# Reordering the places of an attention layer from chunk, head, node to head, node, chunk, with output products of 40 columns

## The chip, the cores and the metric

The kernel runs on one core of a Trainium2 chip. The time of a run is the device time in microseconds of one execution of the whole program. Four runs of the kernel before the change took 7528.65, 7554.27, 7571.19 and 7575.57 us, with a median of 7562.73 us.

## The reference

The program computes four graph layers with normalizations and residuals on 6250 nodes and 100,000 edges, all in fp32. Edges are sorted by destination. The change touches only layer 0, the attention layer, whose core is this (cut):

```python
msg_s = (s_n @ Ws_src)[src] + (s_n @ Ws_dst)[dst]
msg_v = einsum(v_n, Wv_src)[src] + einsum(v_n, Wv_dst)[dst]
w1 = rbf @ W_rbf
m1_s, m1_v = _cg_tp(msg_s, msg_v, y0, y1, w1...)
a = leaky(m1_s @ W_alpha), per head: sum(a * alpha_dot)
ex = exp(a - segment_max(a, dst)[dst])
den = segment_sum(ex, dst); alpha = ex / den[dst]
val_s, val_v = gated projections of m1_s, m1_v
m2_s, m2_v = _cg_tp(val_s, val_v, y0, y1, w2...)
h = per head: [m2_s @ Ws_vlin, m2_v @ Wv_vlin]       # 16 + 8*3 = 40 numbers of each head
agg = segment_sum(alpha * h, dst)
```

A message is formed for each edge, each of 4 heads scores it, and each destination node takes a softmax over its edges and adds up the 40 numbers of each head with the weights of the softmax.

## The kernel before

Edges are cut into 784 chunks of 128; 4 chunks are one window, so there are 196 windows (class `Window0`, from L1545). As edges are sorted, the destinations of a chunk lie within 16 consecutive nodes from a base node that is known per chunk (`WM0 = 16`). A pair of chunks uses the 128 partitions as *places*: one partition for each combination of chunk of the pair (2), head (4) and node (16). Before the change partition 64 x chunk + 16 x head + node is the place, so a chunk has a contiguous half (`S = 64`).

What one window goes through, with the lines that matter here:

- **Loads.** The base nodes of the chunks are read into registers of SyncE (`bases`). The rows of their 16 destination nodes (`nodes`, L1584, tile `fw`) come by four DMAs, one for each chunk, to the first 16 rows of a quarter of 32 partitions. Rows of the source nodes come by indirect DMAs from GpSimd (L978, tile `f`). For groups of four windows, `ends_load` brings the destination numbers (tile `dn`) on SyncE's queue, and `radial_load` brings the radial inputs (tiles `yr`, `yb`) on ScalarE's queue.
- **Masks.** `masks` compares the destination numbers with the node of each place (`on`, 1 where the edge belongs to the place).
- **Messages.** `ends` (L1602) multiplies the mask of a chunk, 16 rows of it, with its 16 node rows: this spreads node rows over edges, into PSUM tile `wf`. `weights` (L1607) puts the radial weights beside them. `features` and the four pieces of `product1` (L1623, L1625, L1627, L1629, all on VectorE, reading `wf`) form the tensor product `tp`.
- **Projections.** `turn` transposes (L1650) into a PSUM bank `m` (four such banks rotate), `turned` copies (ScalarE, L1655, tile `xt`), `linear` multiplies (L1662), `tanh`, `directed`, `gates`, `values`, `gated`, `crossed` and `joined` make the values `val`.
- **Scores.** `channels` (L1720), `leak`, `leaky`, `scores` (L1733) with the matrix `adot` give every place a score for every edge. `largest` (VectorE, L1742) takes the maximum over edges; the tile `row` (42 numbers for each place and pair) starts here. `exps` (ScalarE, L1758, one instruction for each pair) makes the weights `pT`, with places on partitions and edges along the free axis. `denominators` (VectorE, L1765) adds them up into column 40 of `row`.
- **Sums.** `by_edge` (L1771) transposes the weights so that edges are on partitions. `weighted` (VectorE, L1778, tile `py`) multiplies them with the four spherical harmonics. `sums` (L1786) multiplies with the scalar values, `sums_z` (L1799) with the vector values, and `summed` (ScalarE, L1791, twice, tile `a`) and `summed_z` (ScalarE, L1807, tile `az`) copy the results to SBUF, channels on partitions and places along the free axis.
- **Outputs.** `outputs` (L1818) applies the last linear map for each pair: 5 groups of channels times 4 blocks of 32 places, so 20 fp32 products for a pair and 40 for a window. Each works on 32 columns of the array, has 32 places of `a` or `az` as the loaded weights, and streams `w_o`. A block of 32 places holds two heads, so `w_o` has 80 columns, 40 for each, and half of the 80 results are of the wrong head.
- **Rows.** `even` (ScalarE, L1823) and `odd` (VectorE, L1827) pick the right 40 by multiplying with a mask `own` and its complement. `write` (SyncE, L1841) stores the 64 partitions of a chunk to a table in HBM, where later code merges the chunks.

An fp32 product appears in the trace as two passes: two records of a weight load (LDWEIGHTS) and two of a product (MATMUL).

The order of the work is written by hand. Stage s of the loop goes through the list `STEP0` (L1899 to L1913) and does every operation named there for window s - lag, in a block in which the program's order is kept on each engine:

```python
for lag, name, *arg in STEP0:
    if 0 <= s - lag < NST:
        getattr(ws[s - lag], name)(*arg)
fill()
```

`fill` issues one DMA of zeros for later tables at the end of a stage. SyncE's queue in a stage is: register loads, node rows, the loads of `ends_load` (every fourth stage), then the four `write`s and `fill`. [...]

Of the kernel before, what the change touches and what calls it, by code (L numbers as in the profile page):

```python
# [48 lines left out]
def kernel(ctx: ExitStack, tc: tile.TileContext, t: dict, out: bass.AP):  # L49
# [230 lines left out]
    slot0 = const.tile([P, 2], F32, name="slot0")  # L280
    win0B = const.tile([1, NW0], I32, name="win0B")
    lane0 = const.tile([P, 1], F32, name="lane0")
    with tc.tile_pool(name="win", bufs=1) as sb, tc.tile_pool(name="winp", bufs=1, space=PSUM) as ps:
# [155 lines left out]
        vec.tensor_scalar(bits[:, 0:1], pi, 15, None, ALU.bitwise_and)  # L439
        vec.tensor_scalar(bits[:, 1:2], pi, 6, None, ALU.logical_shift_right)  # L440
        vec.tensor_scalar(bits[:, 2:3], pi, 5, 1, ALU.logical_shift_right, ALU.bitwise_and)
        vec.tensor_scalar(bits[:, 3:4], pi, 4, 1, ALU.logical_shift_right, ALU.bitwise_and)
        bf = sb.tile([P, 4], F32, name="bf")
        vec.tensor_copy(bf, bits)
        vec.tensor_scalar(bf[:, 2:3], bf[:, 2:3], 2.0, bf[:, 3:4], ALU.mult, ALU.add)
        vec.tensor_scalar(slot0[:, 0:1], bf[:, 1:2], float(WM0), bf[:, 0:1], ALU.mult, ALU.add)
        vec.tensor_scalar(slot0[:, 1:2], bf[:, 2:3], float(NROWS), slot0[:, 0:1], ALU.mult, ALU.add)
        bd = sb.tile([P, NCH], F32, name="bd")
# [6 lines left out]
        for g in range(4):  # L455
            q = slice(32 * g, 32 * g + 32)
            vec.tensor_copy(win0F[q, :], nb[q, g // 2 : NCH : 2])
# [1089 lines left out]
    class Window0:  # L1547
# [12 lines left out]
        def __init__(self, w, sb, ps, n, k, radial, dst, gi, y, yc, ids, node_idx, rows, tps):  # L1560
            self.w, self.sb, self.ps, self.n, self.np = w, sb, ps, n, n // 2
            self.k, self.radial, self.dst = k, radial, dst
            self.gi, self.y, self.yc, self.ids, self.node_idx = gi, y, yc, ids, node_idx
            self.rows, self.tps = rows, tps
            self.first, self.radial_next = True, None
            self.t, self.z, self.pa = {}, {}, {}
            self.f = self.xt = self.th = self.q = self.val = self.a = self.pz = self.po = None

            self.groups = [(g, c) for g, c in enumerate(ORDER0) if c < n]
# [7 lines left out]
        def nodes(self):  # L1577

            self.fw = self.sb.tile([P, F], F32, name="fw", bufs=4)
            if self.rows is None:  # L1580
                gather(self.fw, feat[1][:, :], self.node_idx)
                return
            for g, c in self.groups:
                nc.sync.dma_start(self.fw[32 * g : 32 * g + WM0, :], feat[1][ds(self.base[c], WM0), :])  # L1584
# [11 lines left out]
        def ends(self):  # L1596
# [3 lines left out]
            for g, c in self.groups:  # L1600
                q = slice(32 * g, 32 * g + WM0)
# [151 lines left out]
        def exps(self, old=None):  # L1753
# [3 lines left out]
            for p in range(self.np):  # L1757
                act.activation(self.pT[:, p, :], s[:, p, :], AF.Exp, bias=neg[:, p : p + 1])  # L1758
# [3 lines left out]

        def denominators(self):
            m = self.np
            vec.tensor_reduce(self.row[:, 0:m, 40], self.pT[:, 0:m, :], AX.X, ALU.add)  # L1765

        def by_edge(self):

            self.pe = self.bank()
            for p in range(self.np):  # L1770
                pe.transpose(self.pe[:, p * P : (p + 1) * P], self.pT[:, p, :], ident)  # L1771
# [16 lines left out]
        def summed(self, p):  # L1788
            if self.a is None:
                self.a = self.sb.tile([P, 2, 2, 8, 32], F32, name="a", bufs=2)  # L1790
            act.copy(self.a[:, p], self.pa[p].rearrange("p (h k m) -> p h k m", h=2, k=8))  # L1791
# [11 lines left out]
        def summed_z(self):  # L1803
            m = self.np
            self.az = self.sb.tile([P, 2, 4, 32], F32, name="az", bufs=2)
            z = self.pz[:, 0 : 4 * S].rearrange("p (h k m) -> p h k m", h=2, k=4)[:, :, 0 : 2 * m]
            act.copy(self.az[:, :, 0 : 2 * m], z)  # L1807

        def outputs(self, p):

            w = self.w["o"]
            if self.po is None:
                self.po = self.bank()[:, 0:160].rearrange("p (a k) -> p a k", a=2)
            for i in range(5):
                for r in range(4):
                    h, g = r // 2, r % 2
                    x = self.a[:, p, h, 2 * i + g] if i < 4 else self.az[:, h, 2 * p + g]
                    pe.matmul(self.po[32 * r : 32 * r + 32, p, :], x, w[:, i, g, :], start=i == 0, stop=i == 4)  # L1818

        def even(self):  # L1820

            m = self.np
            act.activation(self.row[:, 0:m, 0:40], self.po[:, 0:m, 0:40], AF.Copy, scale=self.w["own"][:, 0:1])  # L1823

        def odd(self, old=None):
            m, row = self.np, self.row
            vec.scalar_tensor_tensor(  # L1827
                row[:, 0:m, 0:40], self.po[:, 0:m, 40:80], self.w["own"][:, 1:2], row[:, 0:m, 0:40], ALU.mult, ALU.add
            )
            if old is not None:  # L1830
                vec.scalar_tensor_tensor(row[:, 0, 0:41], old[:, 0:41], self.keep, row[:, 0, 0:41], ALU.mult, ALU.add)
# [7 lines left out]
        def write(self, c):  # L1839
            k, h = self.rows[0][c], c % 2  # L1840
            nc.sync.dma_start(tabs[0][k][0][:, ds(self.base[c], WM0), :], self.row[h * S : (h + 1) * S, c // 2, :])  # L1841
# [42 lines left out]
    class Ends:  # L1884
# [5 lines left out]
        def load(self):  # L1890
            n = self.dst[0].shape[1]
            self.dn = self.sb.tile([P, self.m, P], self.dst[0].dtype, name="dn", bufs=2)
            for h in range(2):
                nc.sync.dma_start(self.dn[h * S : (h + 1) * S, 0:n, :], self.dst[h].to_broadcast([S, n, P]))
# [4 lines left out]
        (3, "dots"), (3, "dot", 1), (1, "edges", 0), (3, "dot", 2), (1, "edges", 1), (0, "bases"), (0, "nodes"),  # L1899
# [3 lines left out]
        (4, "turned", 0), (8, "outputs", 0), (4, "tanh", 3), (3, "product1", 1), (8, "even"), (3, "product1", 2),  # L1903
        (4, "channels"), (5, "gates"), (4, "leak"), (3, "product1", 3), (4, "directed", 3), (0, "ends_load"),
        (2, "ends"), (5, "crossed"), (5, "joined", 0), (0, "edges", 2), (5, "joined", 1), (0, "edges", 3), (8, "odd"),
# [535 lines left out]
```

## Time and profile before

One execution was profiled. Its span is the time from the first to the last instruction of the trace.

| what | value |
|---|---|
| median of four runs | 7562.73 us |
| profiled execution | 7578.01 us |
| its span | 7576.2 us |
| TensorE products, busy | 6278.6 us (83%) |
| VectorE busy | 5082.5 us (67%) |
| ScalarE busy | 3030.6 us (40%) |
| GpSimd busy | 4214.0 us (56%) |
| mean granted clock of TensorE | 0.874 |
| loop of layer 0, outputs (L1818) of first and last window | 343.8 to 2461.5 us of the span |
| distance of the outputs of neighbouring stages | 10.9 us |

PE stands for TensorE's products, PEld for its weight loads, which overlap them, DVE for VectorE, ACT for ScalarE, POOL for GpSimd and SP for SyncE. A line of the timeline or of the groups names the line of the program, the operation, its output and inputs by tile name, then the sizes; for TensorE "128\*32 128x80" means rows by columns of the array that are used and the moving data's partitions by columns. "x32" counts instructions. A "<-" in a wait names what ended it; "issue" is time in which the engine waited for nothing that the profile shows.

### The profile page before, as it was taken

The numbers are of one execution on the slowest core, as the hardware profiler recorded it, in microseconds if no ns is written. First come the engines' busy times: TensorE is split into PE (matmuls) and PEld (weight loads), VectorE is DVE, ScalarE is ACT, GpSimd is POOL, SyncE is SP. The second block draws the span as 40 slices with busy tenths as digits, with TensorE's granted clock in tenths as the row PEclk, the third lists the DMA queues.
The fourth block names the chain that finished last, engine by engine and source line by source line (L and its number), as shares of the span: only waits on it lengthen the run. The fifth ranks groups of instructions, "written<-read, shape, count | busy, mean of one in ns | idle before, by whom it ended". The sixth has DMA issues, their size and how long they took to land. (4 is left out here: it accounts for less than half of the span.)

```text
span 7576.2 us, 188755 instructions
## 1 busy us (share of the span) xinstructions
PE 6278.6 (83%) x69706; PEld 4869.4 (64%) x69706; DVE 5082.5 (67%) x12849; ACT 3030.6 (40%) x8425; POOL 4214.0 (56%) x4019
## 2 busy tenths in 40 slices
PE   1799999999999799999999567777777677777776
PEld 0687878878888688888888444444455444444454
DVE  5688889888988788888888544444444334444444
ACT  0455555555555566666666421111111101111112
POOL 0355655655554387877888435545454345454443
PEclk9999999999999899999999767777777777777777
DMA  4444444444432677777777633333333333333333
GB/s 139 123 104 101 103 101 105 102 102 105 102 86 52 131 134 124 128 127 124 129 123 116 177 93 99 87 101 91 101 92 102 95 90 111 94 110 94 109 101 91
DMA packets 772958, 814.43 MB, mean 107 GB/s; under 512 B 187424, under 2 KB 634529, under 8 KB 770337
## 3 DMA queue, kind: packets, MB, share of 16 engines
q1 hardware_dynamic: 498016, 504.14, 22.5%
q0 software_dynamic: 225792, 269.95, 21.5%
q10 hardware_dynamic: 48192, 27.91, 1.5%
q8 instruction: 562, 9.21, 0.5%
q14 instruction: 396, 3.24, 0.1%
HBM read 524.80 MB, written 276.70 MB: 106 GB/s over the span
## 5 line engine op out<-in xcount | busy, mean ns | idle before, releaser
L978 POOL DMA_INDIRECT f<-feat,r_src x2352 | 2322.4, 987 | 1959.7 <-issue 503.2
L1397 POOL DMA_INDIRECT tab<-o,scat x784 | 1385.2, 1767 | 429.9 <-issue 111.1
L1130 PE MATMUL pa<-pr,oy 128*32 128x160 f32 (+4 forms) x15680 | 998.3, 294 | 621.3 <-issue 609.5
L1130 PEld LDWEIGHTS pa<-pr,oy 128*32 128x32 f32 x15680 | 600.0, 123 | 1121.4 <-issue 1050.4
L1096 DVE TENSOR_TENSOR wy<-ww,r_y 128x576 f32<-128x576 f32 x131 | 99.0, 756 | 836.6 <-PE ww L1070 503.7
L1104 DVE TENSOR_TENSOR pr<-f,ww 128x384 f32<-128x384 f32 x131 | 72.5, 553 | 863.7 <-PE ww L1070 614.1
L1662 PE MATMUL m<-w_m,xt 128*128 128x128 f32 x4704 | 622.9, 276 | 0.7 <-DVE q L1679 0.4
L1662 PEld LDWEIGHTS m<-w_m,xt 128*128 128x128 f32 x4704 | 588.4, 192 | 11.7 <-ACT xt L1655 1.1
L1136 ACT COPY o<-pa 128x160 f32<-128x160 f32 x262 | 76.5, 292 | 1136.3 <-remote 710.9
L1070 PE MATMUL ww<-w,hid 64*128 64x192 f32 (+1 forms) x2088 | 448.0, 485 | 96.7 <-issue 68.5
L1655 ACT COPY xt<-m 128x384 f32<-128x384 f32 x784 | 356.6, 481 | 413.8 <-PE m L1771 166.8
L1640 POOL TENSOR_TENSOR d<-d 128x128 f32<-128x128 f32 x392 | 203.1, 518 | 499.1 <-DVE d L1636 495.0
L1366 ACT COPY xt<-pt 128x384 f32<-128x384 f32 x784 | 374.5, 482 | 196.1 <-PE pt L1364 168.4
L1138 ACT COPY o<-pa 128x96 f32<-128x96 f32 x262 | 62.2, 237 | 963.3 <-remote 679.7
L1070 PEld LDWEIGHTS ww<-w,hid 64*128 64x128 f32 x2088 | 276.8, 255 | 210.6 <-issue 180.1
L1786 PE MATMUL m<-py,val 128*128 128x256 f32 x1568 | 403.8, 380 | 0.0
L1364 PE MATMUL pt<-ident,tp 128*128 128x128 f32 x2352 | 388.1, 273 | 16.7 <-DVE tp L975 16.0
L1818 PE MATMUL m<-w_o,a 128*32 128x80 f32 x12544 | 351.1, 235 | 61.1 <-issue 61.1
L1374 PE MATMUL lin<-l,xt 128*128 128x160 f32 x1568 | 386.5, 328 | 0.0
L1354 ACT COPY fw<-pf 128x384 f32<-128x384 f32 x784 | 337.8, 484 | 113.8 <-PE pf L1352 96.5
L1650 PE MATMUL m<-ident,tp 128*128 128x128 f32 x2352 | 376.6, 283 | 1.9 <-ACT xt L1655 1.7
L1070 PE MATMUL ww<-w2z,hid 128*128 128x192 f32 (+1 forms) x1048 | 353.7, 471 | 8.4 <-issue 8.1
(424 smaller groups left out, 15229.8 us busy)
## 6 DMA issues: line engine op xcount, KB each, us to landing
tab<-zeros SPq DMA_DIRECT2D x170, 448.0 KB
nodes<-in_src_row_dram SPq DMA_DIRECT2D x392, 128.0 KB
f<-feat,r_src POOLq DMA_INDIRECT x2352
tb<-tab SPq DMA_DIRECT2D x20, 1288.0 KB
tb<-tab SPq DMA_DIRECT2D x20, 1280.0 KB
dn<-in_dst_row_dram SPq DMA_DIRECT2D x98, 256.0 KB
dn<-in_dst_row_dram SPq DMA_DIRECT2D x196, 128.0 KB
e<-in_ef64T_dram SPq DMA_DIRECT2D x196, 128.0 KB
```

Of the source, the lines that this page charges most:

```text
L978: pool.indirect_dma_start(out=o, out_offset=None, in_=table, in_offset=bass.IndirectOffsetOnAxis(ap=idx, axis=0),)
L1070: pe.matmul(self.ww[:, q, 0:wn], self.hid[k, c * P : (c + 1) * P], m, start=True, stop=True)
L1130: pe.matmul(o, self.oy[:, q, r], x, start=c + piece == 0, stop=c == self.ns[h] - 1 and piece == len(ps_) - 1)
L1364: pe.transpose(pt[:, k, :], self.tp[:, c, k * P : (k + 1) * P], ident)
L1366: act.copy(self.xts[c], pt)
L1374: pe.matmul(z[:, 64:224], xt[:, 2, :], w["l3"], start=True, stop=False)
L1397: pool.indirect_dma_start(out=self.tables[c % len(self.tables)], out_offset=bass.IndirectOffsetOnAxis(ap=self.scat[:, c : c + 1], axis=0), ...
L1650: pe.transpose(pt[:, k * P : (k + 1) * P], self.tp[:, c, k * P : (k + 1) * P], ident)
L1655: act.copy(self.xt[:, :, c, :], self.t[c][:, 0 : 3 * P].rearrange("p (k e) -> p k e", k=3))
L1662: pe.matmul(z[:, k, :], self.xt[:, k, c, :], self.w["m"][:, k, :], start=True, stop=True)
L1786: pe.matmul(pa[:, h * 256 : (h + 1) * 256], self.val[:, c, 0:P], py, start=True, stop=True)
L1818: pe.matmul(self.po[32 * r : 32 * r + 32, p, :], x, w[:, i, g, :], start=i == 0, stop=i == 4)
```

## The change

Places are put in the order head, node, chunk: partition 32 x head + 2 x node + chunk of the pair. A block of 32 places now belongs to one head, with the two chunks of the pair side by side.

- `outputs`: `w_o` is [128, 5, 4, 40] in place of [128, 5, 2, 80]. The number of products stays at 40 for each window; each streams 40 columns. The results are already the right ones, so `even` becomes a plain copy, `rows_out`, and `odd` and `own` go.
- `denominators` goes; `exps` has ScalarE's exponentials add up along the free axis as they run (`accum_out`).
- The transposes of `by_edge` store their columns in the order chunk, head, node, as what follows expects. `summed` and `summed_z` store places with chunks interleaved, so every second element.
- `ends` uses all 32 rows of a quarter. `fw` becomes four fixed tiles, set to zero once; the node rows of a chunk go to every second partition. `write` and the loads of `ends_load` address every second partition as well.
- In `STEP0`, `bases` and `nodes` move from the front of the list to behind `ends_load` and `radial_load`.
- Preparation: positions of the places are worked out anew (`slot0`, `win0F`), and `adot` is put together by two VectorE copies in place of two DMAs.

The code below is the core of the diff; a path for windows left over after the loop changes in the same way and is left out.

```diff
         def nodes(self):
...
+            self.fw = next(self.fws)
             for g, c in self.groups:
-                nc.sync.dma_start(self.fw[32 * g : 32 * g + WM0, :], feat[1][ds(self.base[c], WM0), :])
+                nc.sync.dma_start(
+                    self.fw[32 * g + c % 2 : 32 * g + 32 : 2, :], feat[1][ds(self.base[c], WM0), :]
+                )
...
             for g, c in self.groups:
-                q = slice(32 * g, 32 * g + WM0)
+                q = slice(32 * g, 32 * g + 32)
                 pe.matmul(self.wf[:, c, 0:F], self.on[q, c // 2, :], self.fw[q, :], start=True, stop=True)
...
-                act.activation(self.pT[:, p, :], s[:, p, :], AF.Exp, bias=neg[:, p : p + 1])
+                act.activation(
+                    self.pT[:, p, :], s[:, p, :], AF.Exp, bias=neg[:, p : p + 1], accum_out=self.row[:, p, 40:41]
+                )
...
-        def denominators(self):
-            m = self.np
-            vec.tensor_reduce(self.row[:, 0:m, 40], self.pT[:, 0:m, :], AX.X, ALU.add)
-
         def by_edge(self):
 
             self.pe = self.bank()
             for p in range(self.np):
-                pe.transpose(self.pe[:, p * P : (p + 1) * P], self.pT[:, p, :], ident)
+                o = self.pe[:, p * P : (p + 1) * P].rearrange("q (h m) -> q m h", h=2)
+                pe.transpose(o, self.pT[:, p, :], ident)
...
         def summed(self, p):
             if self.a is None:
-                self.a = self.sb.tile([P, 2, 2, 8, 32], F32, name="a", bufs=2)
-            act.copy(self.a[:, p], self.pa[p].rearrange("p (h k m) -> p h k m", h=2, k=8))
+                self.a = self.sb.tile([P, 2, 16, 32], F32, name="a", bufs=2)
+            o = self.a[:, p].rearrange("p k (n h) -> p h k n", h=2)
+            act.copy(o, self.pa[p].rearrange("p (h k n) -> p h k n", h=2, k=16))
...
         def summed_z(self):
             m = self.np
-            self.az = self.sb.tile([P, 2, 4, 32], F32, name="az", bufs=2)
-            z = self.pz[:, 0 : 4 * S].rearrange("p (h k m) -> p h k m", h=2, k=4)[:, :, 0 : 2 * m]
-            act.copy(self.az[:, :, 0 : 2 * m], z)
+            self.az = self.sb.tile([P, 8, 32], F32, name="az", bufs=2)
+            z = self.pz[:, 0 : 4 * S].rearrange("p (h k n) -> p h k n", h=2, k=8)[:, :, 0 : 4 * m]
+            act.copy(self.az[:, 0 : 4 * m].rearrange("p k (n h) -> p h k n", h=2), z)
...
-                self.po = self.bank()[:, 0:160].rearrange("p (a k) -> p a k", a=2)
+                self.po = self.bank()[:, 0:80].rearrange("p (a k) -> p a k", a=2)
             for i in range(5):
                 for r in range(4):
-                    h, g = r // 2, r % 2
-                    x = self.a[:, p, h, 2 * i + g] if i < 4 else self.az[:, h, 2 * p + g]
-                    pe.matmul(self.po[32 * r : 32 * r + 32, p, :], x, w[:, i, g, :], start=i == 0, stop=i == 4)
-
-        def even(self):
+                    x = self.a[:, p, 4 * i + r] if i < 4 else self.az[:, 4 * p + r]
+                    pe.matmul(self.po[32 * r : 32 * r + 32, p, :], x, w[:, i, r, :], start=i == 0, stop=i == 4)
+
+        def rows_out(self):
 
             m = self.np
-            act.activation(self.row[:, 0:m, 0:40], self.po[:, 0:m, 0:40], AF.Copy, scale=self.w["own"][:, 0:1])
-
-        def odd(self, old=None):
-            m, row = self.np, self.row
-            vec.scalar_tensor_tensor(
-                row[:, 0:m, 0:40], self.po[:, 0:m, 40:80], self.w["own"][:, 1:2], row[:, 0:m, 0:40], ALU.mult, ALU.add
-            )
...
+            act.copy(self.row[:, 0:m, 0:40], self.po[:, 0:m])
...
-            nc.sync.dma_start(tabs[0][k][0][:, ds(self.base[c], WM0), :], self.row[h * S : (h + 1) * S, c // 2, :])
+            nc.sync.dma_start(tabs[0][k][0][:, ds(self.base[c], WM0), :], self.row[h:P:2, c // 2, :])
...
-                nc.sync.dma_start(self.dn[h * S : (h + 1) * S, 0:n, :], self.dst[h].to_broadcast([S, n, P]))
+                nc.sync.dma_start(self.dn[h:P:2, 0:n, :], self.dst[h].to_broadcast([S, n, P]))
...
     STEP0 = [
-        (3, "dots"), (3, "dot", 1), (1, "edges", 0), (3, "dot", 2), (1, "edges", 1), (0, "bases"), (0, "nodes"),
+        (3, "dots"), (3, "dot", 1), (1, "edges", 0), (3, "dot", 2), (1, "edges", 1),
...
-        (4, "turned", 0), (8, "outputs", 0), (4, "tanh", 3), (3, "product1", 1), (8, "even"), (3, "product1", 2),
+        (4, "turned", 0), (8, "outputs", 0), (4, "tanh", 3), (3, "product1", 1), (8, "rows_out"), (3, "product1", 2),
...
-        (2, "ends"), (5, "crossed"), (5, "joined", 0), (0, "edges", 2), (5, "joined", 1), (0, "edges", 3), (8, "odd"),
-        (0, "radial_load"), (2, "weights"), (3, "turn", 3), (8, "write", 0), (4, "leaky"), (6, "by_edge"),
-        (3, "turned", 3), (4, "linear", 0), (7, "sums", 1), (4, "tanh", 0), (7, "denominators"), (7, "summed", 1),
+        (2, "ends"), (5, "crossed"), (5, "joined", 0), (0, "edges", 2), (5, "joined", 1), (0, "edges", 3),
+        (0, "radial_load"), (0, "bases"), (0, "nodes"), (2, "weights"), (3, "turn", 3), (8, "write", 0), (4, "leaky"), (6, "by_edge"),
+        (3, "turned", 3), (4, "linear", 0), (7, "sums", 1), (4, "tanh", 0), (7, "summed", 1),
```

## The prediction

> **What bounds the kernel now.** I looked first at the clock and the busy shares of long windows, to see which part of the span the change can reach. Columns: window, its length, then busy time with number of instructions for TensorE products (PE), weight loads (PEld), DVE, ACT and POOL, then the granted TensorE clock, the DMA share and GB/s.
>
> ```profile
> 500.00:2400.00 1900.00, 1837.62 (x31133) 1520.82 (x31127) 1703.51 (x5359) 1069.78 (x3285) 1128.40 (x1427) 1.00 0.42 98
> ...
> 2462.00:7576.00 5114.00, 4088.17 (x33897) 3054.34 (x33897) 2987.48 (x6190) 1764.13 (x4563) 2928.50 (x2352) 0.82 0.49 110
> ```
>
> The loop of layer 0 fills the first window and ends at 2461.5 us; all that the change touches, but for some preparation, is there: 196 stages of about 10.9 us, 28% of the span. The second window is code that stays as it is, so I cost it at nothing. In the loop PE is busy 97% (1837.6 of 1900), DVE 90%, ACT 56%, at full clock. PE looks like the bound, but a busy PE is not a PE at its peak, so the waits in the same window come next (engine, tile, line <- what ended the wait: total us, times, longest).
>
> ```profile
> ACT row L1823 <- PE m L1818: 270.0, 172, 1.9
> ...
> PEld m L1818 <- issue: 116.7, 346, 0.8
> ...
> DVE py L1778 <- PE m L1771: 102.4, 150, 0.9
> ...
> PE m L1818 <- issue: 56.2, 173, 0.6
> ```
>
> TensorE stops once in every stage (173 stages) inside the output products, L1818, and no semaphore ends the stop. The timeline of one stage shows where (start, length, engine, ..., idle before).
>
> ```profile
> 1408.97 0.59 ACT L1791 COPY a<-m 128x512 f32<-128x512 f32 x1 [0.52 <-PE m L1786]
> ...
> 1409.86 0.76 PE L1818 MATMUL m<-w_o,a 128*32 128x80 f32 x32
> ...
> 1410.44 0.32 PE L1818 MATMUL m<-w_o,az 128*32 128x80 f32 x8
> ...
> 1410.58 0.31 PE L1818 MATMUL m<-w_o,a 128*32 128x80 f32 x4
> 1410.63 0.55 DVE L1627 TENSOR_TENSOR tp<-f,wf 128x384 f32<-128x384 f32 x1
> ...
> 1411.24 0.71 PE L1818 MATMUL m<-w_o,a 128*32 128x80 f32 x26 [0.36 <-issue]
> ...
> 1412.08 0.65 PE L1720 MATMUL m<-xt,w_alpha 128*64 128x256 f32 x4
> ```
>
> Of the 80 passes (40 fp32 products of two passes), 44 run by 1410.65, nothing starts until 1411.24, then 36 run. Over some 155 stages the restart comes 0.07 us after the end of DVE's L1627, with nine stages in ten inside a band of 0.08 us, while its distance from the products' own start spreads from 1.21 to 1.48 us (10th to 90th percentile). So the restart goes with the DVE chain, not with how soon the first 44 passes are done. No wait of the program says so; I don't know the mechanism, and that is the largest doubt here. With it the stage is a loop: L1720 at 1401.16, the transposes L1771, DVE's py L1778 at 1403.78 (2.62 later), a chain of DVE work without a gap to the end of L1627 at 1411.17 (7.39), restart, 36 passes and the change of tile shape to L1720 at 1412.08 (0.91): 10.92 us.
>
> **The change part by part.**
>
> *Output products, 80 to 40 columns.* The number of passes and weight loads stays. The price per pass I take from two groups of the same shape of weights (128*32). The first 32 passes of the outputs above take 0.76 us with the last pass's own 0.235: (0.76 - 0.235)/31 = 16.9 ns from start to start. For 64 columns there is L1799:
>
> ```profile
> 1416.19 0.65 PE L1799 MATMUL m<-py,val 128*32 128x64 f32 x32
> ```
>
> (0.65 - 0.222)/31 = 13.8 ns. So 3.1 ns for 16 columns, 0.19 ns per column, and 40 columns would be 9.3 ns if the line holds that far. Were all 80 passes on the path, this gives 80 x 7.6 = 0.61 us per stage, 119 us. But by the loop above only the 36 after the restart are. They take 0.68 us from first start to last. The first four come about 20 ns apart, as the queue fills again, and I leave those 0.08; the other 32 take 0.30 at 9.3 ns (gain 0.30), 0.44 at the 13.8 ns that the trace has shown to be possible (gain 0.16), and 0.51 at 16 ns, the pace of the weight loads just after the restart (gain 0.09). I take 0.22, between the first two: 196 x 0.22 = **43 us**. Bounds in this case: 18 to 59 us.
>
> [...]
>
> *Work taken from DVE.* L1765 (414 ns) and L1827 (298 ns) go: 0.71 us per stage, 140 us in all. Both stand outside the chain from L1778 to L1627: before L1778 DVE waits for PE anyway (102.4 us in 173 stages). I cost them at nothing. If that wait were gone, they would be worth up to those 140 us.
>
> *Work put on ACT.* The rows that bear on it, by form (count | busy us, mean ns):
>
> ```profile
> L1791 ACT COPY a<-m 128x512 f32<-128x512 f32 x346 | 202.7, 586 | 168.3 <-issue 90.9 <-PE m L1786 75.4 <-PE m L1733 1.0
> ...
> L1758 ACT ACTIVATE pT<-s,neg 128x128 f32<-128x128 f32 x346 | 120.4, 399 | 0.0
> ...
> L1742 DVE DVE_READ_ACCUMULATOR2_ANT row<- 128x1 f32 x346 | 28.6, 83 | 0.2
> ```
>
> The two exponentials now also sum. No ACT row shows that: from 0 to a second pass of 399 ns each; nearest is DVE's read of its accumulator, 83 ns, so 0.17 us per stage. Behind them on ACT stand L1807, which frees a PSUM bank that PE takes at least 0.33 us later, and the xt copies. 0.17 is hidden, 0.8 would not be. The interleaved stores of L1791 and L1807 (every second element) cost 0 to a doubling (0.59, 0.36); 0 is nearest, as their time goes by elements. L1791 ends 0.30 us before the outputs start, and the stop in the outputs covers 0.5 more. L1823 becomes a plain copy, 328 ns or less; it sits in ACT's 270 us of waiting.
>
> *Transposes L1771.* Two per stage, 109 ns apart, on the loop. They now store to PSUM in a strided order, which no row shows: 0 to four times the step, +0.65 us. I take 0, since their elements are the same.
>
> *L1602 with 32 rows in place of 16.* L1607 has 32 rows and 224 columns, mean 347 ns; L1602 16 rows and 160 columns, 346 ns. Rows cost nothing there.
>
> *Transfers and order.* The loads of bases and node rows move behind the ends and radial loads. On SP they pass only the dn loads (1.4 us, every fourth stage); the radial loads are issued by ACT. SP is at work some 7 of 10.9 us, node rows are issued about 14 us before use, so nothing. [...] Loads and stores to every second partition: same bytes and rows, 0 to some tenths of a us on transfers with microseconds to spare. Preparation changes by a few operations once, under 5 us.
>
> **Sum.** -43 us against the profiled execution's 7578.0 us: 7535. That execution lies 15 us over the median of the four runs (7562.7), so for a median I forecast **7522 us**.
>
> **Rivals.**
>
> *The restart moves with the products (gain of the whole).* If the stop comes after a number of passes and has a length, it starts earlier when the passes are shorter. For: its start follows the products' start more tightly than anything of DVE. Against: its end does not. Then 80 passes gain 0.55 to 0.65 us, 108 to 128: about 7445 by the median. Chance 0.22.
>
> *The stop vanishes.* If short passes, or the missing DVE work, take away what causes it, 0.57 us more go, about 235 in all: 7330; a stage can't go below some 9.75 us, as L1602 must wait for DVE's L1629 and the transposes follow. Against: the passes and their number stay. Chance 0.08.
>
> *Nothing is won.* If passes are paced by their issue (16 ns and more after the restart), or ACT's longer exponentials hold PE for as long as the passes save, the time stays: 7545 to 7575. Chance 0.13.
>
> *Slower.* The strided store of the transposes. L1771 lies between the outputs and L1778, with no cover. Each of its two may rise from 109 ns by d; the gain is eaten at 2d = 0.22, so from a step of twice the old one and up the kernel loses; at four times it is +0.65 - 0.22 = 0.43 us per stage, +84 us: 7647. For: PE's stores in this pattern appear in no row. Against: the same elements leave the array. Chance 0.11.
>
> **How the numbers follow.** The forecast's case has 0.46 and reaches from 7505 to 7550. To leave out no more than 2 in 10, the range takes in the whole gain and no gain, 7425 to 7585, and leaves out the vanished stop (0.08) and the strided loss (0.11). A change under 0.5% (38 us) is about what can't be told from none here. The forecast's case, at 18 to 59 us, gives faster 0.27 and same 0.19; with the second and third cases faster is 0.57; no gain adds 0.11 to same and 0.02 to slower; slower is 0.13.
>
> **What would show it.** Right: passes of L1818 nearer 10 than 17 ns apart before and after the stop, the stop still there but longer (about 0.9 us), its end still at L1627's end, stage about 10.7 us. Second case: stop about as long as now, earlier, stage 10.3. Third case: passes after the restart still 16 ns or more apart, or PE waits on ACT az or a. Slower: L1771's step over 200 ns and longer waits of DVE py. Wrong altogether: a new wait of PE on ACT, or layers 1 to 3 taking a different time.

## The result, and the profile after

The changed kernel took **7566.81 us** (median of 52 runs, 7521.30 to 7608.02) against 7552.43 for the kernel before (78 runs, 7521.67 to 7596.18): ratio **1.0018**, 95% interval 1.0008 to 1.0027. Its profiled execution took 7580.33 us with a span of 7578.6. A gain of 43 us was forecast; there is none. The experiments were run in five groups, and in three of them, once on a chip on which another group had taken 7.6 ms, the kernel before took 6.43 ms in place of 7.5 to 7.6, so every ratio below is taken against the kernel before in the same group.

The long windows of the changed kernel, in the columns that the prediction explains (lengths, busy PE, PEld, DVE, ACT, POOL, clock, DMA share, GB/s):

```profile
500.00:2400.00 1900.00, 1760.89 (x30741) 1429.18 (x30741) 1589.88 (x4956) 1071.01 (x3589) 1114.93 (x1410) 1.00 0.39 98
2462.00:7576.00 5114.00, 4078.51 (x34491) 3054.47 (x34488) 2996.14 (x6217) 1776.80 (x4599) 2929.56 (x2356) 0.82 0.49 111
```

Layers 1 to 3 (second line) do the same work at the same clock: 4078.5 us of PE against 4088.2. In the loop of layer 0 PE is busy 76.7 us less than before and DVE 113.6 us less, as the narrower products and the removed work should give. But the loop isn't shorter: a stage takes 11.09 us on average against 10.97. The saved time has become idle time. The waits of the same window (engine, tile, line <- what ended the wait: total us, times, longest) say where:

```profile
PE m L1823 <- issue: 99.3, 234, 0.8
DVE py L1783 <- PE m L1776: 89.2, 124, 1.1
...
DVE s L1748 <- PE m L1739: 38.4, 65, 1.0
...
DVE py L1783 <- PE m L1791: 32.8, 13, 2.6
...
PEld m L1739 <- issue: 20.9, 53, 1.2
DVE q L1683 <- ACT th L1673: 20.4, 32, 0.9
```

L1823 is the old L1818. Its stop grew from 56.2 to 99.3 us and from 173 to 234 times. VectorE's waits for the scores (L1748) are new, those for the tanh (L1683) were 1.4 us before, and py, L1783, now also starts long after its own transposes: the line that names L1791 as the releaser counts 13 starts so late that other products had ended by then, with waits of up to 2.6 us. One stage's timeline (start, length, engine, line, operation, idle before):

```profile
1414.03 0.49 PE L1823 MATMUL m<-w_o,a 128*32 128x40 f32 x32
...
1414.41 0.24 PE L1823 MATMUL m<-w_o,a 128*32 128x40 f32 x3
...
1414.94 0.54 DVE L1633 TENSOR_TENSOR tp<-f,wf 128x384 f32<-128x384 f32 x1
...
1415.03 0.21 PE L1823 MATMUL m<-w_o,a 128*32 128x40 f32 x1 [0.38 <-issue]
...
1415.76 0.49 PE L1823 MATMUL m<-w_o,a 128*32 128x40 f32 x27 [0.52 <-issue]
...
1416.27 0.65 PE L1726 MATMUL m<-xt,w_alpha 128*64 128x256 f32 x4
```

The first 43 passes (eight of az, not shown, between them) have started 0.4 us after the first; before, 44 took 0.8. Then TensorE stops twice (0.38 and 0.52 us idle) where it stopped once.

The prediction's loop can be measured in the trace, step by step, as means over 158 stages. The right two columns are two experiments below: the columns alone, and the whole change with contiguous transfers.

| step of a stage, ns | before | after | before_40 | after_plain_dma_2 |
|---|---|---|---|---|
| last restart inside the outputs to L1720 (after: L1726) | 850 | 523 | 508 | 526 |
| to the second transpose, L1771 (L1776) | 1940 | 1939 | 1940 | 1939 |
| to the start of py, L1778 (L1783) | 621 | 538 | 364 | 312 |
| to the end of L1627 (L1633), DVE's chain | 7500 | 7957 | 7619 | 7716 |
| idle time of DVE within that chain | 118 | 516 | 208 | 293 |
| to the last restart inside the outputs | 82 | 164 | 142 | 73 |
| sum | 10,994 | 11,120 | 10,574 | 10,566 |

The forecast's gain is there (first row, -327 ns). py comes 83 sooner too, though unevenly: 138 of 170 starts are on time (0.31 us), 32 are late by 1.2 us on average. DVE's chain gives it all back (+457, of which 398 are idle time), with 82 more in the last step.

### The profile page after: what moved, and what is told of

Same layout as the page of the kernel before. It is cut to its first block, busy times and chain, and to the rows that moved or that the text cites. A ratio compares the mean times of both kernels' runs of the same rounds, so it can differ in the third digit from the quotient of the medians.

```text
span 7578.6 us, 188884 instructions
## 1 busy us (share of the span) xinstructions
PE 6193.1 (82%) x69706; PEld 4778.8 (63%) x69706; DVE 4975.2 (66%) x12460; ACT 3048.5 (40%) x8817; POOL 4213.2 (56%) x4020
## 5 line engine op out<-in xcount | busy, mean ns | idle before, releaser
L1791 PE MATMUL m<-py,val 128*128 128x256 f32 x1568 | 403.8, 380 | 0.0
L1656 PE MATMUL m<-ident,tp 128*128 128x128 f32 x2352 | 379.1, 283 | 15.2 <-DVE q L1685 11.9
L1783 DVE TENSOR_TENSOR py<-m,r_y 128x1024 f32<-128x1024 f32 x196 | 240.0, 1225 | 182.8 <-PE m L1776 102.6
```

The lines of the kernel that those rows point to most:

```text
L1656: pe.transpose(pt[:, k * P : (k + 1) * P], self.tp[:, c, k * P : (k + 1) * P], ident)
L1791: pe.matmul(pa[:, h * 256 : (h + 1) * 256], self.val[:, c, 0:P], py, start=True, stop=True)
```

## The experiments

Two theories at first. **Supply:** TensorE's instructions come at a limited rate, short passes only use up a store of them sooner, and the time returns as stops. **Store and transfer patterns:** the narrower columns do gain, and something that was costed at nothing takes the gain away: strided stores, strided transfers, ScalarE's sums or the new order.

| kernel | before in that group, us | ratio, 95% interval | us per stage |
|---|---|---|---|
| after_split | 7628.64 | 1.0026 [1.0004, 1.0047] | 11.15 |
| before_40 | 7628.64 | 0.9892 [0.9865, 0.9919] | 10.55 |
| after_dve_sums | 7628.64 | 1.0029 [1.0006, 1.0052] | 11.11 |
| after_80 | 7628.64 | 1.0202 [1.0147, 1.0258] | 11.85 |
| after_again | 7545.25 | 1.0011 [0.9993, 1.0029] | 11.03 |
| after_old_order_2 | 7545.25 | 1.0047 [1.0030, 1.0063] | 11.13 |
| after_plain_dma_2 | 7545.25 | 0.9902 [0.9879, 0.9925] | 10.56 |
| after_old_order | 6428.72 | 0.9985 [0.9972, 0.9999] | 10.23 |
| before_40_order | 6428.72 | 0.9901 [0.9885, 0.9918] | 9.91 |
| after_plain_stores | 6428.72 | 0.9907 [0.9891, 0.9924] | 10.03 |
| after_plain_dma | 6428.72 | 0.9889 [0.9867, 0.9910] | 9.89 |
| after_plain_fw | 6427.80 | 0.9881 [0.9865, 0.9898] | 9.85 |
| after_plain_writes | 6427.80 | 0.9918 [0.9902, 0.9935] | 10.03 |
| after_joined_last | 6427.80 | 0.9908 [0.9891, 0.9924] | 10.02 |
| before_joined_last | 6427.80 | 0.9996 [0.9987, 1.0006] | 10.24 |
| after_joined_last_2 | 6426.63 | 0.9916 [0.9900, 0.9933] | 10.03 |
| after_plain_fw_2 | 6426.63 | 0.9869 [0.9852, 0.9886] | 9.86 |

The kernel before has 10.94 to 10.97 us per stage in its profiles at 7.5 ms; before_joined_last, equal to it in time, has 10.24 at 6.4 ms.

### Columns, sums, and a supply of instructions

**before_40** is the kernel before with 40 of its 80 columns streamed (the core of the edit; `odd` reads the same 40):

```diff
-  pe.matmul(self.po[32 * r : 32 * r + 32, p, :], x, w[:, i, g, :], ...)
+  pe.matmul(self.po[32 * r : 32 * r + 32, p, 0:40], x, w[:, i, g, 0:40], ...)
```

> The kernel before, with 40 of the 80 columns streamed in every output product and both row instructions reading those 40 (half of the outputs' results are left out). Only the column count differs. Theory F: the first 40 passes take 0.3 us less but the end of the last stop comes no sooner; the tail of 36 passes takes 0.2 us less. Outputs 0.2 us per stage shorter. If what the change lost elsewhere (0.36 us per stage around the scores and sums_z) comes from ScalarE's accumulation, it is absent here: 0.993 to 0.995. If it comes from the stops being moved to other sections of the stage, it is here too: 0.999 to 1.003. Theory D: 0.993 to 0.996.

0.9892, by the interval 62 to 103 us less, more than either theory had. The columns alone gain: 0.42 us per stage between the profiles, or 82 us in the loop. By the table of steps 0.34 comes from the passes after the restart, as forecast in kind, and 0.26 from py, which starts sooner; 0.18 is lost again in DVE's chain and before the restart.

**after_80** is the changed kernel with columns padded back to 80 by zeros (the core of the edit):

```diff
-  wo = o5 = wp.tile([P, 5, 4, 40], F32, name="w_o")
+  wo = wp.tile([P, 5, 4, 80], F32, name="w_o")
+  o5 = wo[:, :, :, 0:40]
```

> The changed kernel with the output products padded to 80 columns with zero weights, so that every pass is as long as before and all else is as after. If the columns won 0.2 us per stage and other parts of the change lost as much: 1.006 to 1.008 of before. If the columns win nothing in the end (theory F with stops that move): 1.000 to 1.003.

1.0202 [1.0147, 1.0258], above both ranges. The rest of the change thus costs some 2% without the columns, and beside the 1.0018 of the changed kernel the columns are worth some 1.8% within it. Its py starts 1.31 us after the second transpose on average, with 48% of the starts over 0.8 us late.

**after_dve_sums** gives the sums of the exponentials back to VectorE (cut):

```diff
-  accum_out=self.row[:, p, 40:41]
+  (7, "denominators")   # VectorE, as before
```

> The changed kernel with the denominators back on VectorE (a reduction of 0.41 us per stage) and no accumulation in ScalarE's exponentials (no accumulator reads, 0.39 us per stage less on ScalarE). If the accumulation costs the time that the columns won: 0.990 to 0.995 of before. If it lies beside other work: 1.000 to 1.003, as the changed kernel.

1.0029, as the changed kernel: ScalarE's sums away and 0.4 us more of VectorE change nothing together. Each by itself wasn't tried.

**after_split** moves the second half of the outputs ahead of linear 3 and turn 0, so that other products stand between the two halves:

```diff
-  (5, "tanh", 2), (5, "directed", 1), (4, "linear", 3), ... (4, "turn", 0), (8, "outputs", 1),
+  (5, "tanh", 2), (8, "outputs", 1), (5, "directed", 1), (4, "linear", 3), ... (4, "turn", 0),
```

> The changed kernel with the two halves of the output products set apart: the products of pair 1 come ahead of one projection (linear) and one group of transposes (turn) of about 1.3 us together, those of pair 0 stay. Same instructions, order alone. Theory F (supply): TensorE has a reserve of instructions that is used up after some 40 passes at full pace, and fetches more one request at a time, about 0.69 us each, each asking only for what had been used when it was sent. Then each half of 40 passes fits the reserve, the stops of 0.13 to 0.6 and 0.69 us in the outputs go, and two more changes of tile shape (0.1 us each) come: 0.6 to 0.9 us less per stage, 115 to 175 us, 0.977 to 0.985 of before. Theory D (the restart goes with the chain of VectorE): the second half cannot end sooner than that chain lets it, so the stop moves into another place; no gain, or up to 40 us more for the tile shapes, 1.000 to 1.007 of before.

1.0026. The supply theory, taken as a store that refills during other products, promised a gain (0.977 to 0.985) and failed: outputs, linear 3 and turn 0 together take 3.04 us against 3.02, and the transposes L1656 after L1805 have a new stop (1.12 us in place of 0.71). The stop that was driven from one place turned up in another here.

### Order and stores

**after_old_order** puts `bases` and `nodes` back at the front of the list, and **before_40_order** gives before_40 the new order (the edit shown is that of after_old_order, the other is its reverse):

```diff
-  (0, "radial_load"), (0, "bases"), (0, "nodes"), (2, "weights"),
+  (1, "edges", 1), (0, "bases"), (0, "nodes"), ...   (0, "radial_load"), (2, "weights"),
```

> The changed kernel with the old order of loads (bases and node rows at the front of the list). [...] If the order is harmless: 1.000 to 1.004.

> The kernel before with 40 of 80 columns streamed (half of the outputs' results are left out) and, of the rest of the change, only the new order of the loads. [...] If the order is harmless: 0.987 to 0.992, as with 40 columns alone.

**after_plain_stores** stores the results of the transposes and ScalarE's copies a and az contiguously:

```diff
-  o = self.pe[:, p * P : (p + 1) * P].rearrange("q (h m) -> q m h", h=2)
-  pe.transpose(o, self.pT[:, p, :], ident)
+  pe.transpose(self.pe[:, p * P : (p + 1) * P], self.pT[:, p, :], ident)
...
-  act.copy(o, self.pa[p].rearrange("p (h k n) -> p h k n", h=2, k=16))
+  act.copy(self.a[:, p], self.pa[p].rearrange("p (k n) -> p k n", k=16))
```

> The changed kernel with ScalarE's copies a and az and the transposes of by_edge stored in plain order (places come out mixed up, all sizes the same). Theory S (strided stores give the gain back): 0.990 to 0.995 of before. ScalarE's copies take 635 ns in place of 586, 389 in place of 364; if that lies beside other work: 1.000 to 1.004.

**after_plain_dma** has all three kinds of transfers contiguous again:

```diff
-  self.fw[32 * g + c % 2 : 32 * g + 32 : 2, :]
+  self.fw[32 * g : 32 * g + WM0, :]
-  self.row[h:P:2, c // 2, :]
+  self.row[h * S : (h + 1) * S, c // 2, :]
-  self.dn[h:P:2, 0:n, :]
+  self.dn[h * S : (h + 1) * S, 0:n, :]
```

> The changed kernel with node rows, row stores and destination loads addressed to contiguous partitions as before the change (places come out mixed up; same bytes and same count of transfers). Theory T (transfers to every second partition land later and hold ScalarE's and SyncE's queues through the DMA semaphores): 0.990 to 0.995 of before, and the radial loads issued without the wait of 0.2 to 1.2 us. If not: 1.000 to 1.004.

These four ran at 6.43 ms, where all but after_old_order gain 0.9 to 1.1%. The new order doesn't look like what costs: the columns with it gain 0.9901 (before_40 itself wasn't run at 6.43 ms), and the changed kernel with the old order is the one without the gain (0.9985, just below the range expected). after_plain_stores and after_plain_dma can't be read without the changed kernel itself at 6.43 ms, and it wasn't run there. So the same question was put again, with both kernels beside it.

### The transfers, at 7.5 ms

> The kernel before as it is, for a profile on the chip of this call. The chip of the second call ran all kernels in 6.35 to 6.43 ms and its stops in the outputs were 0.1 to 0.2 us; the other chips 7.5 to 7.7 ms with stops of 0.6 to 0.7. Theory F (supply of instructions, with a latency that belongs to the chip): on a chip like the second the outputs of the kernel before take about 1.4 us (80 passes at 17 ns), on one like the first 2.0 us.

> The changed kernel, as a control beside before on this chip. On a chip like the first: 1.001 to 1.003 of before. On one like the second theory F leaves no stop that eats the columns' gain: 0.985 to 0.993. If the chip does not matter: 1.001 to 1.003 on either.

> The changed kernel with the old order of loads, beside the control. Theory R (the new order holds ScalarE and gives the gain back): 0.006 to 0.010 below the control. The second call points against it (0.9985 where other variants have 0.989 to 0.991): then the same as the control or up to 0.01 above it.

> The changed kernel with transfers to contiguous partitions, beside the control. Theory T (transfers to every second partition cost time through the waits of their issuers): 0.005 to 0.012 below the control. If they cost nothing: the control's ratio within 0.002.

These runs settle the part. after_again repeats the result (1.0011). With contiguous transfers and nothing else altered the ratio is **0.9902**, as with the columns alone (0.9892). The old order makes it worse (1.0047): the new place of the loads, which I had taken for neutral, is worth 0.4% to the changed kernel. The waits of the window 500 to 2400 us in after_plain_dma_2:

```profile
DVE py L1783 <- PE m L1776: 121.1, 167, 2.7
PE m L1823 <- issue: 82.1, 185, 0.5
...
PEld m L1739 <- issue: 7.8, 17, 0.9
```

and in after_again:

```profile
DVE py L1783 <- PE m L1776: 95.1, 131, 1.2
PE m L1823 <- issue: 94.9, 224, 0.7
...
DVE py L1783 <- PE m L1791: 30.5, 12, 2.6
PEld m L1739 <- issue: 19.9, 45, 1.3
```

Contiguous transfers take away the very late starts of py (the line with L1791 goes; the 2.7 us that is left lies in the last stage of this loop, which ends inside the window), 12.8 of PE's 94.9 us inside the outputs, and 12.1 of the 19.9 before the scores, L1739. By the steps of the loop (after_again to after_plain_dma_2): py -185 ns, DVE's chain -222 (its idle time -206), the last step -84, in all -484 ns. DVE idles in its chain ahead of L1748 (276 ns per stage in after_again, 154 in after_plain_dma_2, 38 in before_look), which reads the scores, and ahead of L1683 (189, 105 and 19), which follows the tanh.

What TensorE itself loses is seen in the distance of its sections (means, after_again to after_plain_dma_2): L1823 1929 to 1771 ns, L1805 806 to 627, L1739 625 to 544. One stage of after_plain_dma_2, from the transposes on:

```profile
1406.56 0.38 PE L1776 MATMUL m<-ident,pT 128*128 128x128 f32 x2
...
1406.98 1.22 DVE L1783 TENSOR_TENSOR py<-m,r_y 128x1024 f32<-128x1024 f32 x1 [0.71 <-PE m L1776]
...
1407.24 0.47 POOL L1699 TENSOR_TENSOR q<-q 128x128 f32<-128x128 f32 x1
```

and a late one of the changed kernel:

```profile
1418.10 0.38 PE L1776 MATMUL m<-ident,pT 128*128 128x128 f32 x2
...
1418.61 0.46 POOL L1699 TENSOR_TENSOR q<-q 128x128 f32<-128x128 f32 x1
...
1419.34 1.23 DVE L1783 TENSOR_TENSOR py<-m,r_y 128x1024 f32<-128x1024 f32 x1 [1.53 <-PE m L1668]
```

In the first, py starts 0.04 us after the transposes' end, and GpSimd's addition L1699 (L1693 in the kernel before) comes later. In the second, py starts 0.86 us after that end, when the addition is over, and ends at 1420.57; TensorE's L1805 needs it and starts at 1420.77. In the kernel before, 71% of the starts come 0.5 to 0.8 us after the second transpose's start, in place of 0.31, and the addition then begins about when py is due and ends about when py starts. The two go together closely: the addition begins no later than 0.15 us after py is due in all of the late starts (130 in the kernel before, 28 in after_again) and in 8 of 43 and 7 of 144 that are on time. The addition's own length doesn't cover the long waits: in the second fence it was over 0.27 us before py started.

### Which transfer, and GpSimd's addition

**after_plain_fw** undoes the stride of the node rows alone, **after_plain_writes** that of the row stores alone (the matching lines of the diff above). **after_joined_last** and **before_joined_last** put the last gather ahead of GpSimd's addition, so that the addition comes behind the start of py:

```diff
-  (5, "joined", 1), (0, "edges", 3),
+  (0, "edges", 3), (5, "joined", 1),
```

> The changed kernel with only the node rows loaded to 16 contiguous partitions (places come out mixed up; same bytes, same count). In the traces the issue of one such load takes 525 to 580 ns on SyncE where the contiguous one takes 316. If this part of the addressing gives the columns' gain back: 0.990 to 0.994 of before, with L1699 of GpSimd no longer ahead of py. If it is the row stores or the destination loads: 1.000 to 1.003.

> The changed kernel with only the row stores taken from 64 contiguous partitions (the stored rows are mixed up; everything inside the loop computes on the same data as in the changed kernel). Their issue takes 621 ns where the contiguous one takes 562, 0.2 us per stage. If the row stores give the gain back: 0.990 to 0.994. If it is the node rows: 0.999 to 1.003.

> The changed kernel, order alone: on GpSimd the second half of joined (L1699) comes behind the last gather in place of ahead of it. Theory G (py on VectorE is held, by 0.35 to 1.9 us, whenever L1699 of GpSimd starts before py can): py starts 0.31 us behind the transposes in every stage, 0.18 us per stage less, 0.993 to 0.997 of before. If the delay of py has another cause: 1.000 to 1.003, with py late in over a tenth of the stages as before.

> The kernel before with the same swap on GpSimd. There py is late by 0.35 us in seven of ten stages. Theory G: py always 0.31 us behind the transposes, 0.2 to 0.3 us per stage less, 0.991 to 0.995 of before. Otherwise 0.999 to 1.002.

> Again the changed kernel with L1699 of GpSimd behind the last gather, since the call before ran in the fast condition (before at 6428 us), where py was late in no stage of any kernel. In the slow condition (before at some 7550 us) theory G: py 0.31 us behind the transposes in every stage, where the changed kernel has 0.49 us on average and over 0.8 us in 12% of the stages; 0.2 us per stage less, 0.995 to 0.998 of before (changed kernel: 1.001 to 1.002). Otherwise 1.001 to 1.003. In the fast condition: 0.990 to 0.992 again.

> Again the changed kernel with only the node rows loaded to contiguous partitions. In the slow condition: 0.990 to 0.993 of before if the node rows carry what all three kinds of transfers together give (0.990 there), 1.000 to 1.003 if it is the destination loads or the row stores. In the fast condition: 0.987 to 0.990 again.

Both groups came at 6.43 ms, where py is on time in every one of these kernels (0.31 us after the second transpose). So nothing here tests whether GpSimd's addition holds py; that stays open. The transfers can be told apart, with after_joined_last in the place of the changed kernel (the swap did nothing to the kernel before, 0.9996): contiguous node rows 0.9881 and 0.9869, contiguous row stores 0.9918, neither (after_joined_last) 0.9908 and 0.9916. The node rows are the part that costs there, 0.17 us per stage. At 6.4 ms TensorE's stops go with their issue: in four kernels with strided node rows TensorE's stops in the outputs add up to 72 ns in the 35 stages without a node-row issue near the first half of the outputs, and to 181 to 241 ns in the groups of stages where one overlaps it. With contiguous node rows it is 20 and 56 ns. Outputs of after_plain_fw, with the issue of node rows beside them:

```profile
1409.69 3.16 SPq L1588 DMA_DIRECT2D fw<-feat  x4
...
1410.64 0.49 PE L1823 MATMUL m<-w_o,a 128*32 128x40 f32 x32
...
1411.02 0.59 PE L1823 MATMUL m<-w_o,a 128*32 128x40 f32 x31
```

All 80 passes run without a stop, 0.9 us from the first start to the last, as in 125 of 160 stages of this kernel. At 7.5 ms the same count doesn't show it: the stops add up to 1.06 us in the 31 stages of after_again without a node-row issue near, and to 0.96 in the 123 others.

The split of the loss between the three transfers at 7.5 ms wasn't tried. The traces show where it sits. In every fourth stage GpSimd multiplies `yr` by `yb` some 3 us ahead, its addition then comes 0.2 us later, and py is late in none of these stages, in the kernel before (0 of 43, but all 130 of the others) as in after_again. These stages take 10.70 us in after_again against 10.50 in after_plain_dma_2, a loss near that of the node rows at 6.4 ms; the other three of each four take 11.17 against 10.59. How much of this larger loss goes with GpSimd's addition and how much with a transfer, isn't known.

## Why the prediction was wrong, step by step

- **"Loads and stores to every second partition: same bytes and rows, 0 to some tenths of a us on transfers with microseconds to spare."** This is the step that failed. I counted bytes and landing times and priced what is left at nothing; the stage pays 0.48 us. Undone, the strides give 1.1% (1.0011 to 0.9902), as much as the columns gain: TensorE's stops inside the outputs, ahead of the scores and of L1805 are shorter without them, py starts on time, and DVE's chain idles less. That the strided transfers are the cause is shown. How they do it isn't. One thing that they change, and that I didn't price, is the time at issue on SyncE's queue (count: shortest/median/longest, ns):

```profile
L1584 SPq DMA_DIRECT2D fw<-feat x784: 3/316/1850, 276.7 to 2397.3; - x196
```

```profile
L1588 SPq DMA_DIRECT2D fw<-feat x784: 3/534/1657, 279.4 to 2422.2; - x196
```

  The means in the loop are 364 ns before and 553 after, those of a row store 583 and 612: 4 x 0.19 + 4 x 0.03 = 0.9 us more per stage, for which SyncE has time: its queue waits for other work for 480 of the 1900 us from 500 to 2400 after the change, and for 481 before. That this is the path is only argued, from the stops beside the issues at 6.4 ms; at 7.5 ms, where the loss is larger, the stops don't keep to the issues, and by what path an issue would hold TensorE isn't known.
- **"A chain of DVE work without a gap to the end of L1627", 7.39 us.** It was taken as fixed. It has 0.52 us of gaps per stage in place of 0.12, mostly ahead of L1748, which waits for the scores, and L1683. This is where the gain went.
- **"The restart goes with the DVE chain"**, the largest doubt. At 7.5 ms it held in the main: the last restart follows the end of L1627 or L1633 by 73 to 164 ns in the mean in four kernels, and in after_plain_dma_2 by 57 to 91 ns (10th to 90th percentile), but in the changed kernel by 54 to 323. It isn't a law. Outputs of before_joined_last at 6.4 ms, which begin at 1412.52:

```profile
1413.11 0.54 DVE L1627 TENSOR_TENSOR tp<-f,wf 128x384 f32<-128x384 f32 x1
...
1413.23 0.74 PE L1818 MATMUL m<-w_o,a 128*32 128x80 f32 x32
...
1413.78 0.32 PE L1818 MATMUL m<-w_o,az 128*32 128x80 f32 x8
```

  L1627 ends at 1413.65, in the middle of passes that run on without a stop, as in all 160 stages that were counted. So no dependence ties the two; the mechanism stays unknown.
- **36 passes, 0.22 us.** Right in kind, somewhat small: 0.33 by the table. Passes after the last restart are 10.9 ns apart against 19.2, and 9.7 against 18.4 before the first stop, where I took 9.3 from a line through 64 and 80 columns. The section of the outputs fell by 0.235 us in its median (2212 to 1977). The forecast priced the first four passes after the restart at 0.08 us by a queue that fills again; no run shows such a queue, and in the traces these four come 22 ns apart before and 21 after (medians of 172 and 170 stages).
- **What follows when a stall goes.** I hadn't seen py's late start as part of the loop. before_40 gains 0.26 us there, more than half of its result, which no step of mine has.
- **Removed DVE work at nothing** and **ACT's accumulation hidden:** nothing speaks against either, but after_dve_sums tests the two only together. The accumulation was 194 ns for each exponential, not 83. Forms of the changed kernel (count | busy us, mean ns | idle before):

```profile
L1797 ACT COPY a<-m 128x512 f32<-128x512 f32 x392 | 249.0, 635 | 188.4 <-PE m L1791 78.6 <-issue 64.0 <-PE m L1739 44.4
...
L1764 ACT ACTIVATE pT<-s,neg 128x128 f32<-128x128 f32 x392 | 153.7, 398 | 0.0
...
L1764 ACT ACTIVATION_READ_ACCUMULATOR pT<-s,neg 128x1 f32 x392 | 76.1, 194 | 0.0
```

  The interleaved copies take 635 and 389 ns against 586 and 364, a twelfth more at most, far from a doubling.
- **Strided transposes at 0:** right; the step from one to the other is 109 ns at L1776 as it was at L1771. The slow rival, built on a step of over 200 ns for one transpose, falls.
- **Order of the loads at nothing:** not for strided transfers, where the old place is worse (1.0047 against 1.0011). For contiguous ones before_40_order (0.9901 at 6.4 ms, against 0.9892 with the old order at 7.6) shows no loss, but the two weren't run side by side.
- **The rivals.** The time fell into "nothing is won" (7545 to 7575), but by neither of its mechanisms: passes are 10.9 ns apart after the stop, and no gain came from taking ScalarE's sums away. That the time lies so near the old one is chance: a gain and a loss of 1.1% each. "The restart moves with the products" gave 7445; the columns alone reach 0.9892, about 7470 from 7552, by another way. "The stop vanishes" happened only at 6.4 ms. No rival was built on transfers.

## What to carry to other kernels

Don't cost a changed DMA pattern at nothing because its landing has slack: with every second partition as its destination a load was half as long again at issue in the mean (553 against 364 ns), on a queue with idle time (480 of 1900 us), and with all three kinds of transfers strided the stage was 0.5 us longer (11.03 against 10.56 us). Before a gain on one engine is counted, walk the whole loop and ask of each link with no slack what else can hold it; here the links "py after the transposes" and "DVE's chain" moved by as much as the change. Where a layout makes the products cheap and the transfers awkward, measure both halves: here they are worth 1.1% each. With strided transfers no version beat the kernel before at 7.5 ms, though after_joined_last did by 0.8 to 0.9% at 6.4. Places in the order head, chunk, node would keep the 40 columns and give the node rows of a chunk 16 neighbouring partitions again; this wasn't tried.

## What the runs showed of the hardware

- The same program ran at 7.5 to 7.6 ms in two groups of runs, as in the runs first shown, and at 6.43 ms in three. Most of the difference lies outside the loop. Layers 1 to 3 of the kernel before, first from before_look, in the group at 7545 us (window 2462 to 7500, then the largest group of products with its idle time):

```profile
2462.00:7500.00 5038.00, 4040.03 (x33744) 3023.63 (x33744) 2956.66 (x6105) 1750.25 (x4531) 2913.60 (x2344) 0.82 0.47 111
```

```profile
L1130 PE MATMUL pa<-pr,oy 128*32 128x160 f32 (+4 forms) x15680 | 994.6, 294 | 644.5 <-issue 637.0 <-remote 4.3 <-DVE oy L1079 0.4
```

  and the same from before_joined_last, at 6428 us:

```profile
2462.00:7500.00 5038.00, 3365.93 (x33455) 2722.64 (x33455) 2914.43 (x6037) 1724.53 (x4429) 2937.61 (x2340) 0.92 0.47 109
```

```profile
L1130 PE MATMUL pa<-pr,oy 128*32 128x96 f32 (+4 forms) x15680 | 566.7, 270 | 0.0
```

  The idle time ahead of the products that nothing in the profile explains ("issue") is 637 us in one and nothing in the other, and the granted clock of the window is 0.82 and 0.92. Its cause isn't known; inside the loop, at clock 1.00, the same stops of TensorE shrink or go.
- The stop of TensorE in the outputs has a last part of much the same length, median 0.67 to 0.70 us from one pass to the next, in the six profiles at 7.5 ms with 40 columns and the outputs in one piece, and 0.1 to 0.2 us or none at 6.4. It comes after 43 or 44 passes in the median, whether these take 9.7 or 19 ns. A limited supply of TensorE's instructions would look like that, but after_split speaks against a simple store. Nor do the transfers of instructions that the trace holds (in the kernel before 221 of 16 KB on queue 8 from 500 to 2200 us, 1.4 for each stage) keep step with a stop that comes once in each: the end of the nearest lies 1.8 us from the restart in the median. The cause stays open.
- VectorE's py starts late beside GpSimd's addition (by 0.35 us in most stages of the kernel before, by 0.8 and more in some 12 to 16% of the stages of the changed one). The traces show the coincidence: in the kernel before all 130 late starts have the addition beside them, and no start is late in the 43 stages where it comes 0.2 us later. But no run moved the addition alone at 7.5 ms, so whether it holds py isn't decided.
